# Half-width output tiles on TensorE in a graph-and-experts kernel: the last 53 destinations of an attention layer, and the overflow rows of a mixture of experts

## The chip, the cores and the metric

The kernel runs on one core of one Trainium2 chip. The time is the device time of one execution in microseconds (us). Of the engines, PE is TensorE (matmul; "PEld" is its loading of weights), DVE is VectorE, ACT is ScalarE, POOL is GpSimd and SP issues DMAs. Line numbers (L1273) are those of the kernel before.

## The reference, cut to what matters

There are 3125 nodes with 256 features, 103,125 edges (50,000 pairs in both directions and one loop per node), and four layers, each added to its input after a layer norm:

```python
x = x + gat3(ln(x))          # three graph attention layers: softmax over edges
x = x + moe16(ln(x))         # 16 experts, each token goes to its top 2
x = x + relu(xn @ W + segment_sum((xn @ M)[src], dst))
x = x + moe8(ln(x))          # 8 experts, one per token

# one attention layer of gat3
e = leaky_relu(el[src] + er[dst]); ex = exp(e - max)
out = segment_sum(ex / sum * h[src], dst)

# moe16
top_probs, top_idx = top_k(softmax(x @ gate), 2)
out = sum over the two experts of p * ((silu(x @ w1) * (x @ w2)) @ w3)   # hidden width 512
```

With the fixed inputs the 16 experts of `moe16` get 473, 306, 378, 384, 428, 407, 354, 351, 470, 372, 338, 459, 390, 379, 405 and 356 rows (6250 in all, worked out from the reference). Seven of them have more than 384 rows, and three of those have more than 448.

## The kernel before

All matmuls named here are in fp32. One fp32 matmul of the program shows as two instructions (two passes) in the profile, so counts of PE instructions are twice the matmuls. The Tile scheduler writes each engine's order; it may interleave pieces of neighbouring steps, but an engine works through its own order strictly.

**Attention (`dense_attention`).** The edges are held as a dense table of counts, sources on 128 partitions (25 tiles `s`), destinations along the row. Destinations are worked in 13 groups (`GROUPS`): twelve of 256 and a last one of 53. For each group and each `s`, DVE makes `pm` = max(tau, rho) times the counts (L1270), and PE multiplies it, as the stationary operand, with the node features `h` of that source tile (257 columns, L1273), one matmul for each 128 destinations, summed over `s` in PSUM (`acc`). `pm` has six buffers, so DVE runs up to six tiles ahead. What follows a group is put into a list `later` and issued inside the next group's loop at fixed `s`: `divide` (L1291 to L1300), and then, in layers 1 and 2, `onward` (transposes at L1313, the next layer's projection at L1113). In layer 3 the router follows instead: `norm`, `gate` and `send` (L613 to L674), which end in an indirect DMA that scatters each row to its expert's place in DRAM (`rows`). After the last group the router's `finish` counts each expert's rows and makes a small table of which expert has rows beyond 384, for the next stage.

**First experts (`routed_experts`).** Each of the 16 experts has 384 rows in the main loop: `turn` loads and transposes them (L732, L737), `first` multiplies them by w1 and w2 (weights stationary, 384 rows moving, L762) and makes `hid` = silu times product (L765, L766), and `second` multiplies `hid` by w3 for each 128 rows (L775), scales it (`y`, L778) and adds it into DRAM `sums` by an indirect DMA on POOL (L780). Rows beyond 384 are worked in slots of 128, one slot after each of the experts 3 to 10 (`BETWEEN = 8`), whether a slot has an expert or only the spare tile: `first_more` (transposes L800, matmuls of 128x128 weights with 128 moving rows L807) and `second_more` (L819, scaled at L821, indirect DMA L824). The weights of a slot's expert are loaded again by SP from a table entry that SP reads (L785 to L796), into the same rotating buffers as the main loop's weights. Scatters into `sums` of one expert are free of order among themselves; those of different experts or slots wait for one another. `y` has three buffers. If more slots are needed than `BETWEEN`, a branch at the end works the rest.

**Order at the seams.** The experts' first rows are read only when all scattered rows have landed. `sums` are read back only when the last scatter has landed.

Of the kernel before, what the change touches and what calls it, by code (L numbers as in the profile page):

```python
# [21 lines left out]
P = 128  # L22
N = 3125
NT = 25
# [498 lines left out]
BETWEEN = 8  # L523
# [40 lines left out]
class Router:  # L564
# [115 lines left out]
    def finish(self, cp, pp, over):  # L680
# [11 lines left out]
        nc.vector.tensor_scalar(end[:, 0, NX0:], total, float(EACH * P), None, op0=OP.is_gt)  # L692
        for j in range(4):
            nc.vector.tensor_tensor(end[:, j + 1, NX0:], end[:, j, NX0:], end[:, j, NX0 - (1 << j):-(1 << j)],
                                    op=OP.add)
        end = end[:, 4, NX0:]
        table = self.table
        nc.vector.tensor_scalar(table[:, 2, 0:1], end[:, NX0 - 1:], float(BETWEEN), None, op0=OP.is_gt)
        slot = cp.tile([1, NX0], F32, name="more_slot")
        nc.gpsimd.iota(slot, pattern=[[1, NX0]], base=0, channel_multiplier=0, allow_small_or_imprecise_dtypes=True)  # L700
        done = cp.tile([1, NX0, NX0], BF16, name="more_done")
        nc.vector.tensor_tensor(done, end[:, None, :].to_broadcast([1, NX0, NX0]),
                                slot[:, :, None].to_broadcast([1, NX0, NX0]), op=OP.is_le)
        nc.vector.tensor_reduce(slot, done, AX.X, OP.add)
        nc.vector.tensor_scalar(table[:, 0], slot, float(NX0 - 1), None, op0=OP.min)

        nc.vector.tensor_scalar(slot, slot, float(NP), float(EACH * P), op0=OP.mult, op1=OP.add)
        nc.vector.tensor_scalar(table[:, 1], slot, float(NX0 * NP), None, op0=OP.min)


def routed_experts(tc, x, ident, rows, sums, places, w1, w2, w3, load):
# [10 lines left out]
    with tc.tile_pool(name="rw", bufs=3) as ep, tc.tile_pool(name="rx", bufs=2) as xp, \  # L722
# [46 lines left out]
        def second(e, xs, hid, o):  # L769
            who = xp.tile([P, nq], I32, name="who")  # L770
            nc.gpsimd.tensor_copy(who, xs[:, :, D])
            for q in range(nq):
                ps = po.tile([P, D], F32, name="ps_o")
# [9 lines left out]

        def first_more(slot):
            e = nc.values_load(places[0:1, 0, slot:slot + 1], engines=(mybir.EngineType.SP,), min_val=0,  # L785
                               max_val=NX0 - 1, skip_runtime_bounds_check_because="min with the last expert")
            at = nc.values_load(places[0:1, 1, slot:slot + 1], engines=(mybir.EngineType.SP,), min_val=0,
                                max_val=NX0 * NP, skip_runtime_bounds_check_because="min with the spare tile")
            xs = mp.tile([P, ROW0], F32, name="xs1")
            nc.sync.dma_start(xs, rows[ds(at, P)])  # L790
            a = ep.tile([P, KD, HID0], F32, name="w1")
            nc.sync.dma_start(a, w1[ds(e, 1)].rearrange("o (k p) h -> p (o k) h", p=P))
            b = ep.tile([P, KD, HID0], F32, name="w2")
            nc.sync.dma_start(b, w2[ds(e, 1)].rearrange("o (k p) h -> p (o k) h", p=P))
            o = op_.tile([P, nh, D], F32, name="w3")
            nc.sync.dma_start(o, w3[ds(e, 1)].rearrange("o (k p) f -> p (o k) f", p=P))  # L796
            xsT = mp.tile([P, KD, P], F32, name="xsT1")
            ps = tp.tile([P, KD, P], F32, name="ps_x")
            for k in range(KD):
                nc.tensor.transpose(ps[:, k], xs[:, k * P:(k + 1) * P], ident)  # L800
            nc.scalar.copy(xsT, ps)
            p1 = pp.tile([P, nh, P], F32, name="ps_h1")
            p2 = pp.tile([P, nh, P], F32, name="ps_h2")
            for ps, w in ((p1, a), (p2, b)):
                for j in range(nh):
                    for k in range(KD):
                        nc.tensor.matmul(ps[:, j], w[:, k, j * P:(j + 1) * P], xsT[:, k], start=(k == 0),  # L807
                                         stop=(k == KD - 1))
            hid = mp.tile([P, nh, P], F32, name="hid1")
            for j in range(0, nh, 2):  # L810
                s = sp.tile([P, 2, P], F32, name="silu")
                nc.scalar.activation(s, p1[:, j:j + 2], AF.Silu)
                nc.vector.tensor_tensor(hid[:, j:j + 2], s, p2[:, j:j + 2], op=OP.mult)
            return slot, xs, hid, o

        def second_more(slot, xs, hid, o):
            ps = po.tile([P, D], F32, name="ps_o")
            for j in range(nh):
                nc.tensor.matmul(ps, hid[:, j], o[:, j], start=(j == 0), stop=(j == nh - 1))  # L819
            y = yp.tile([P, D], F32, name="y")  # L820
            nc.vector.tensor_scalar(y, ps, xs[:, D + 1:D + 2], None, op0=OP.mult)  # L821
            who = yp.tile([P, 1], I32, name="who1")
            nc.gpsimd.tensor_copy(who, xs[:, D:D + 1])
            independent(tc, f"more{slot}", nc.gpsimd.indirect_dma_start(  # L824
                out=sums[:, :], out_offset=bass.IndirectOffsetOnAxis(ap=who, axis=0), in_=y, in_offset=None,
                bounds_check=NP + CAP0 - 1, oob_is_err=True, compute_op=OP.add))
# [4 lines left out]
        for e in range(NX0):  # L831
# [5 lines left out]
            more = first_more(e - 3) if 0 <= e - 3 < BETWEEN else None  # L837
            if e + 1 < NX0:
                turned = turn(e + 1)
            second(e, xs, hid, o)  # L840
# [961 lines left out]
```

## Time and profile before

| | us |
|---|---|
| median of 3 runs (1888.27 to 1890.5) | 1888.33 |
| the profiled execution: its own time | 1892.43 |
| its span, first to last instruction | 1890.7 |
| PE busy in the span | 1836.9 (97%) |
| DVE / ACT / POOL busy | 976.8 / 717.0 / 305.1 |
| mean granted TensorE clock | 0.989 |

The profile has a page and several views. In a row of groups, the columns are line, engine, operation, output and inputs with their shapes, count, then busy time in us and the mean of one in ns, and then the idle time of that engine just before, with what released it. For a matmul "128\*53 128x257" is a stationary operand of 128x53 and a moving one of 128x257. In a row of the timeline, the columns are start and length in us, engine, line, operation and count. Matmuls are pipelined, so the length of one (about 0.38 us) is longer than its share of a stream; a stream is better timed from its first start to the next line's start.

The attention layers run from about 72 to 1064 us, the router's end and the first rows to 1083, the first experts from there to 1385.

### The profile page before, as it was taken

The page shows a single profiled execution, that of the slowest core. Times are in us where ns is not written, and L with a number is a line of the kernel's source. Part 1 is how long each engine was busy: PE and PEld are TensorE (multiplying, and loading weights), DVE is VectorE, ACT ScalarE, POOL GpSimd, SP SyncE. Part 2 cuts the span into 40 slices and gives each one's busy share as a digit, 9 for nine tenths or more (in the row PEclk, how much of TensorE's full clock was granted, in tenths as well). Part 3 has the DMA queues.
Part 4 walks back from the last instruction along what each step waited for, and adds up shares of the span by engine and source line. Part 5 has one row for each costly group of instructions (what it writes and reads, how often), then busy time and mean ns, then how long its engine had stood idle before and what let it go on. Part 6 is the DMA issues. An engine that isn't in the chain of part 4 may idle for free. (4 is left out here: it accounts for less than half of the span.)

```text
span 1890.7 us, 27634 instructions
## 1 busy us (share of the span) xinstructions
PE 1836.9 (97%) x9569; PEld 1465.0 (77%) x9569; DVE 976.8 (52%) x2687; ACT 717.0 (38%) x2055; POOL 305.1 (16%) x456
## 2 busy tenths in 40 slices
PE   6999999999999999999999899999989999999997
PEld 4788888887888888788888567777668887555886
DVE  5898888875555555577777522222243222324221
ACT  3767766761011111122222211111138998544221
POOL 4210100000000000133333222323210000122122
PEclk9999999999999999999999899999989999999999
DMA  4111214756000000111111265667430000733664
GB/s 114 32 41 40 71 38 166 292 237 251 1 1 0 1 1 6 41 45 45 46 45 41 91 178 156 213 191 201 104 87 1 1 1 10 246 146 135 220 209 126
DMA packets 104342, 183.08 MB, mean 97 GB/s; under 512 B 10808, under 2 KB 73433, under 8 KB 104160
## 3 DMA queue, kind: packets, MB, share of 16 engines
q1 hardware_dynamic: 72268, 124.31, 19.5%
q0 software_dynamic: 16784, 34.42, 6.7%
q10 hardware_dynamic: 15138, 22.44, 3.7%
q8 instruction: 82, 1.34, 0.3%
q14 instruction: 70, 0.57, 0.1%
HBM read 93.05 MB, written 90.17 MB: 97 GB/s over the span
## 5 line engine op out<-in xcount | busy, mean ns | idle before, releaser
L1273 PE MATMUL acc<-big,pm 128*128 128x257 f32 (+1 forms) x3750 | 863.3, 382 | 1.3 <-DVE pm L1270 1.1
L1273 PEld LDWEIGHTS acc<-big,pm 128*128 128x128 f32 (+1 forms) x3750 | 685.7, 187 | 107.0 <-issue 3.5
L1270 DVE SCALAR_TENSOR_TENSOR pm<-tau,rho,counts 128x256 f32<-128x256 f32 (+1 forms) x975 | 446.2, 470 | 232.5 <-PE acc L1273 227.7
L762 PE MATMUL ps_h<-xsT,w 128*128 128x384 f32 x512 | 167.8, 486 | 0.6 <-ACT xsT L738 0.6
L1392 PE MATMUL acc<-msg,cr 128*128 128x512 f32 (+1 forms) x625 | 157.9, 403 | 0.1
L762 PEld LDWEIGHTS ps_h<-xsT,w 128*128 128x128 f32 x512 | 97.2, 190 | 65.2 <-ACT xsT L738 0.8
L1392 PEld LDWEIGHTS acc<-msg,cr 128*128 128x128 f32 (+1 forms) x625 | 114.7, 185 | 29.2 <-ACT cr L1388 1.2
L1388 ACT ACTIVATE cr<-counts 128x256 fp32r<-128x256 uint8 (+1 forms) x325 | 130.5, 402 | 13.6 <-PE acc L1392 6.7
L1645 ACT CAST counts<-acc_c 128x500 uint8<-128x500 f32 (+1 forms) x155 | 95.9, 677 | 94.6 <-PE acc_c L1635 94.6
L995 PE MATMUL ps_y<-t_wd,hsT 128*128 x480 | 108.8, 380 | 0.3 <-ACT hsT L1023 0.3
L766 DVE TENSOR_TENSOR hid<-silu,ps_h 128x384 f32<-128x384 f32 x64 | 35.5, 554 | 139.2 <-PE ps_h L762 139.2
L765 ACT ACTIVATE silu<-ps_h 128x384 f32<-128x384 f32 x64 | 31.4, 490 | 199.6 <-PE ps_h L762 199.6
L1620 DVE TENSOR_TENSOR ohk<-iota_k,key 128x2016 f16<-128x2016 f16 (+1 forms) x79 | 94.4, 1194 | 22.2 <-PE acc_c L1635 22.1
L995 PEld LDWEIGHTS ps_y<-t_wd,hsT 128*128 128x128 f32 x480 | 88.8, 190 | 11.6 <-ACT hsT L1023 0.5
L780 POOL DMA_INDIRECT sums<-y,who x48 | 74.6, 1554 | 129.5 <-DVE y L778 119.8
L1315 ACT ACTIVATE yT<-ps_m 128x256 f32<-128x256 f32 (+1 forms) x50 | 18.7, 374 | 201.0 <-PE ps_m L1313 200.9
L1614 ACT ACTIVATE ohs<-iota_s,low 128x128 f16<-128x128 f16 x286 | 94.1, 401 | 0.0
L901 PE MATMUL ps_H<-big,t_w 128*128 128x512 f32 (+1 forms) x224 | 93.1, 552 | 0.7 <-ACT H L903 0.5
L775 PE MATMUL ps_o<-w,hid 128*128 128x256 f32 x384 | 86.9, 379 | 0.0
L1635 PEld LDWEIGHTS <-ohs 128*128 128x128 f16 x1250 | 77.7, 98 | 10.9
L1635 PE MATMUL acc_c<-ohk,ohs 128*128 128x125 f16 x1250 | 84.5, 218 | 0.0
L775 PEld LDWEIGHTS ps_o<-w,hid 128*128 128x128 f32 x384 | 71.2, 190 | 8.9
(304 smaller groups left out, 1939.1 us busy)
## 6 DMA issues: line engine op xcount, KB each, us to landing
rows<-empty SPq DMA_DIRECT2D x16, 2564.0 KB, 15.9
w<-in_L_ffn_w_dram ACTq DMA_DIRECT2D x42, 512.0 KB, 7.6
hs<-rows SPq DMA_DIRECT2D x29, 641.0 KB, 4.2
w<-in_L_ffn_w_dram SPq DMA_DIRECT2D x30, 512.0 KB, 4.7
rows<-empty SPq DMA_DIRECT2D x16, 516.0 KB, 5.2
t_wd<-in_L_ffn_Wd_dram SPq DMA_DIRECT2D x8, 1024.0 KB, 11.8
xs<-rows SPq DMA_DIRECT2D x15, 387.0 KB, 5.4
bias<-in_L_ffn_bd_dram SPq DMA_DIRECT2D x30, 128.0 KB
```

Source lines behind the costliest of these rows:

```text
L762: nc.tensor.matmul(ps, w[:, k, j * P:(j + 1) * P], xsT[:, k], start=(k == 0), stop=(k == KD - 1))
L775: nc.tensor.matmul(ps, hid[:, j, q * P:(q + 1) * P], o[:, j], start=(j == 0), stop=(j == nh - 1))
L901: nc.tensor.matmul(ps[:, :n], a[:, k, j * P:(j + 1) * P], xnT[:, k, c:c + n], start=(k == 0), stop=(k == KD - 1))
L995: nc.tensor.matmul(ps, hsT[:, j], d[:, ds(e, 1), j, :].rearrange("p o f -> p (o f)"), start=(j == 0), stop=(j == nh - 1))
L1270: nc.vector.scalar_tensor_tensor(pm[:, :n], tau[:, :n], now.rho[:, s:s + 1], edges[:, s, :n], op0=OP.max, op1=OP.mult)
L1273: nc.tensor.matmul(acc[:r, j, :D + 1], pm[:, q:q + r], now.h[:, s], start=(s == 0), stop=(s == NT - 1))
L1388: nc.scalar.activation(cr[:, :n], edges[:, s, :n], AF.Copy, accum_out=seen[:, a * NT + s:a * NT + s + 1])
L1392: nc.tensor.matmul(acc[:r, j].rearrange("p h d -> p (h d)"), cr[:, q:q + r], msg[:, s].rearrange("p h d -> p (h d)"), start=(s == 0), stop ...
L1614: nc.scalar.activation(far[:, i], self.iota_s, AF.Abs, scale=-1.0, bias=self.low32[:, batch, i:i + 1])
L1620: nc.vector.tensor_tensor(to[:, i:tiles].rearrange("p t (x u) -> p t x u", u=2), iota.rearrange("p (x u) -> p x u", u=2)[:, None].to_broad ...
L1635: nc.tensor.matmul(acc[:, u], ohs[:, i], ohk[:, i, :KEYS], start=(t == 0), stop=(t == TW - 1))
L1645: nc.scalar.copy(to[:, :, d0 % PAIR:d0 % PAIR + whole * WIN].rearrange("p s (u d) -> p u s d", u=whole), acc[:, :whole])
```

## The change

Three things are changed.

1. **Last group.** The 25 matmuls of the last group (53 destinations) write in turn to PSUM partitions 0 to 52 (even `s`) and 64 to 116 (odd `s`). DVE makes the stationary operand for six source tiles at once, in two plain operations (`few`, two buffers), where it made it for one in one fused operation. `divide` then adds the two halves: two ACT copies and two DVE additions more.
2. **Overflow rows.** Slots are of 64 rows, each with its own expert, and are worked two at a time, one on partitions 0 to 63 and one on 64 to 127, after the experts 3, 5, 7, 9 and 11 (`BETWEEN = 5` pairs). The rows are now the stationary operand (64 columns) and the weights move (512 columns). `hid` so comes out with rows on partitions and is transposed by four PE transposes (`turn_more`). Each half is scattered by an indirect DMA of its own, and these no longer carry the mark that frees them of order.
3. **Table and buffers.** The table counts halves (an expert beyond 448 rows takes two), so it has 32 entries. The pair's weights lie in a fixed buffer (`room`), the one that `xnT` of the next layer takes later, and not in the rotating ones.

```diff
+SHARE = P // 2
+SUBS = NX0 * (CAP0 - EACH * P) // SHARE
-BETWEEN = 8
+BETWEEN = 5
...
-        nc.vector.tensor_scalar(end[:, 0, NX0:], total, float(EACH * P), None, op0=OP.is_gt)
+        nc.vector.tensor_scalar(own, total, float(EACH * P + SHARE), None, op0=OP.is_gt)
+        nc.vector.scalar_tensor_tensor(end[:, 0, NX0:], total, float(EACH * P), own, op0=OP.is_gt, op1=OP.add)
...
         def first_more(slot):
...
+            for h, (a, b, o) in enumerate(places_of):
+                k = 2 * slot + h
...
+                nc.sync.dma_start(xs[h * SHARE:(h + 1) * SHARE], rows[ds(at, SHARE)])
...
+                nc.sync.dma_start(a, w1[ds(e, 1)].rearrange("o (k p) h -> p (o k) h", p=P))
...
-            for ps, w in ((p1, a), (p2, b)):
-                for j in range(nh):
-                    for k in range(KD):
-                        nc.tensor.matmul(ps[:, j], w[:, k, j * P:(j + 1) * P], xsT[:, k], start=(k == 0),
-                                         stop=(k == KD - 1))
+            for ps, j in ((p1, 1), (p2, 2)):
+                for k in range(KD):
+                    for of in own:
+                        nc.tensor.matmul(ps[of[0]], xsT[:, k, of[0]], of[j][:, k], start=(k == 0), stop=(k == KD - 1))
+            s = sp.tile([P, HID0], F32, name="silu")
+            nc.scalar.activation(s, p1, AF.Silu)
+            nc.vector.tensor_tensor(s, s, p2, op=OP.mult)
+        def turn_more(slot, xs, s, own):
+            ps = tp.tile([P, nh, P], F32, name="ps_x")
+            for j in range(nh):
+                nc.tensor.transpose(ps[:, j], s[:, j * P:(j + 1) * P], ident)
+            hid = mp.tile([P, nh, P], F32, name="hid1")
+            nc.scalar.copy(hid, ps)
         def second_more(slot, xs, hid, own):
             for j in range(nh):
-                nc.tensor.matmul(ps, hid[:, j], o[:, j], start=(j == 0), stop=(j == nh - 1))
+                for half, _, _, o in own:
+                    nc.tensor.matmul(ps[half], hid[:, j, half], o[:, j], start=(j == 0), stop=(j == nh - 1))
+            for half, *_ in own:
...
-            independent(tc, f"more{slot}", nc.gpsimd.indirect_dma_start(
-                out=sums[:, :], out_offset=bass.IndirectOffsetOnAxis(ap=who, axis=0), in_=y, in_offset=None,
-                bounds_check=NP + CAP0 - 1, oob_is_err=True, compute_op=OP.add))
+                nc.gpsimd.indirect_dma_start(
+                    out=sums[:, :], out_offset=bass.IndirectOffsetOnAxis(ap=who[:SHARE], axis=0), in_=y[:SHARE],
+                    in_offset=None, bounds_check=NP + CAP0 - 1, oob_is_err=True, compute_op=OP.add)
...
-            more = first_more(e - 3) if 0 <= e - 3 < BETWEEN else None
+            more = [first_more((e - 3) // 2)] if e % 2 and 0 <= e - 3 < 2 * BETWEEN else []
...
+                        if n <= P // 2:
+                            if s % SOME == 0:
+                                m = min(SOME, NT - s)
+                                few = sp.tile([P, SOME, n], F32, name="few")
+                                nc.vector.tensor_tensor(few[:, :m], tau[:, None, :n].to_broadcast([P, m, n]),
+                                                        now.rho[:, s:s + m, None].to_broadcast([P, m, n]), op=OP.max)
+                                nc.vector.tensor_tensor(few[:, :m], few[:, :m], edges[:, s:s + m, :n], op=OP.mult)
+                            at = s % 2 * (P // 2)
+                            nc.tensor.matmul(acc[at:at + n, 0, :D + 1], few[:, s % SOME], now.h[:, s], start=(s < 2),
+                                             stop=(s >= NT - 2))
...
+                        if r0 <= P // 2:
+                            both = sp.tile([P, D], F32, name="y1")
+                            nc.scalar.copy(both[:r0], acc[P // 2:P // 2 + r0, 0, :D])
+                            nc.scalar.copy(col[:r0, 1:], acc[P // 2:P // 2 + r0, 0, D:D + 1])
+                            nc.vector.tensor_tensor(both[:r0], acc[:r0, 0, :D], both[:r0], op=OP.add)
+                            nc.vector.tensor_tensor(col[:r0, 1:], weight, col[:r0, 1:], op=OP.add)
```

## The prediction

> **What bounds the kernel now.** First the page: PE is busy for 97% of the span, so a matmul saved counts in full wherever PE's queue does not then wait for something else. The edits lie in two stages. For the last attention groups I read the timeline of PE around the end of layer 1:
>
> ```profile
> 439.72 10.72 PE L1273 MATMUL acc<-big,pm 128*128 128x257 f32 x48
> 450.37 0.44 PE L1313 MATMUL ps_m<-ident,y 128*128 128x128 f32 x2
> 450.74 1.07 PE L1273 MATMUL acc<-big,pm 128*53 128x257 f32 x4
> 451.74 1.14 PE L1113 MATMUL ps_m<-we,yT 128*128 128x258 f32 x4
> 452.81 0.64 PE L1273 MATMUL acc<-big,pm 128*53 128x257 f32 x2
> 453.38 0.44 PE L1313 MATMUL ps_m<-ident,y 128*128 128x128 f32 x2
> 453.75 1.07 PE L1273 MATMUL acc<-big,pm 128*53 128x257 f32 x4
> 454.75 1.14 PE L1113 MATMUL ps_m<-we,yT 128*128 128x258 f32 x4
> 455.82 4.55 PE L1273 MATMUL acc<-big,pm 128*53 128x257 f32 x20
> 460.30 0.43 PE L1221 MATMUL ps_m<-ident,lr 128*128 128x128 f32 x2
> ```
>
> PE has no gap here. The last group has 25 matmuls, 50 passes; 30 stand in the 53-wide rows, so 20 of the first row's 48 are its own too, and they begin at 450.37 - 20 x 0.214 = 446.1 (10.72 / 48 is 0.22 a pass, 0.214 without the tail of the last). The group with its guests takes 460.3 - 446.1 = 14.2 us, of which its own 25 matmuls are 50 x 0.214 = 10.7. A pass of 257 columns is 0.214 us whether 128 or 53 wide: half the array idles.
>
> For the overflow slots I read the same view for expert 3:
>
> ```profile
> 1142.24 0.38 PE L800 MATMUL ps_x<-ident,xs 128*128 128x128 f32 x2
> 1143.22 3.73 PE L807 MATMUL ps_h<-xsT,w 128*128 128x128 f32 x32
> 1151.87 1.89 PE L819 MATMUL ps_o<-w,hid 128*128 128x256 f32 x8
> ```
>
> No gaps again. The first `y` of an expert (L778, DVE timeline) comes at 1148.62 and 1170.29, 21.67 apart with a slot, and at 1334.39 and 1350.55, 16.16 apart without: a slot costs 5.51 us, eight cost 44.1. (Seven have rows.)
>
> **Do half-width tiles overlap?** Everything hangs on this, and the trace has a nearest row: L910 writes fp32 products 32 wide to four strips of partitions in turn.
>
> ```profile
> 1660.74 1.92 PE L910 MATMUL ps_zT<-H,t_wg 128*32 128x512 f32 x16
> ...
> 1662.59 1.09 PE L945 MATMUL ps_rows<-ident,H 128*128 128x128 f32 x8
> ...
> 1670.87 9.61 PE L901 MATMUL ps_H<-big,t_w 128*128 128x512 f32 x22
> ```
>
> L901 shows 9.61 / 22 = 0.437 us for a pass of 512 columns. Sixteen such passes in turn would take 7.0; L910's sixteen take 1662.59 - 1660.74 = 1.85. In tenths of a us, four passes are in flight from 1660.7 and eight overlap at 1661.2: four waves of 0.43. So strips do run together, both passes of fp32 too.
>
> Here a page speaks against it. The Trainium skill, "TensorE: Matmul & The Clock Gate", Part 3, says that a weight load overlaps running matmuls only where the row group differs; halves of columns share their rows. By that rule each wave would bare at least one load, and L1273's 53-wide load has a mean of 0.127 us: 3.3 us for the 26 waves of a group, 2.0 for the 16 of a pair of slots. The same page's strict FIFO would also keep a half's second pass between the two halves. L910 contradicts both as a price: its loads (eight in the first 0.16 us) leave no gap between its waves. I go by the row; by the rule the sum below would be -7 instead of -23 (two layers 2 x 1.8, layer 3 1, slots 5 x 8.4 instead of 44.1).
>
> **Last group, layers 1 and 2.** Twenty-five matmuls become 13 turns of two passes: 26 x 0.214 = 5.6 instead of 10.7, -5.1. In the new PE order the blocks between guests are of 10, 3, 4 and 8 matmuls, which pair to 5 + 2 + 2 + 4 = 13, so nothing more is lost. The Trainium skill, "TensorEngine Tiling (Array Packing)", Key Properties, says that a change of tiling mode drains PE, which speaks against short blocks. The rows above price it: four 53-wide passes take 451.74 - 450.74 = 1.00 where four full ones take 0.87, about 0.15 a change; eight changes, but they are there before too (53 wide among 128 wide), so they cost nothing new.
>
> Is DVE quick enough? Before, 25 operations of 0.27. After, five pairs of plain ones; from L1270 (256 elements 486 ns, 53 elements 274, so 1.04 ns an element over 219) 318 elements are 0.55, together about 4.9 us against 6.9. With two `few` buffers the first twelve tiles are ready before the group starts (both batches stand ahead of `divide` in DVE's order). The third batch stands behind `divide` (1.4 us from 446.19 to about 447.6), so its end is about 2.6 us into the group; PE reaches it at 12 x 0.214 + 0.5 for the transposes = 3.1. Covered by 0.5; without that cover each us late costs one. The last one-tile batch stands on DVE behind the guests' two L1116; it ends some 0.6 before PE needs it. The two ACT copies and two DVE additions (0.36 + 0.2, 0.42 + 0.15) fall in the next layer's first group, before its tenth tile; the tile's `h` is needed at `s` = 24. Nothing. Two layers: -10.2.
>
> **Last group, layer 3.** Here the chain is DVE's, not PE's:
>
> ```profile
> 1063.69 0.19 PE L658 MATMUL ps_z<-g_sel,before 128*128 128x32 bf16 x1
> ...
> 1063.99 0.64 PE L1273 MATMUL acc<-big,pm 128*53 128x257 f32 x2
> ...
> 1067.15 0.41 DVE L626 TENSOR_SCALAR row<-big,g_mv,g_rstd 128x256 f32<-128x256 f32 x1
> ...
> 1074.01 0.23 DVE L667 TENSOR_TENSOR g_to<-g_tf,off 128x1 int32<-128x1 f32 x2
> ```
>
> The last matmul stands behind L658, the ranking of the tiles before, which waits for DVE. When PE's group shrinks, that group's `gate` and `send` are no longer inside it but after: in the new order the last tile's L626 stands behind the previous pair's L667. Counted from the group's start at 1051.0: gate sums at 9.3 (before 9.1), about 24 dependent DVE steps of 0.21 to L667 at 14.3, row at 14.5 where it was 16.1. So about 1.5 of the 5.1 stays, less some ACT table loads (1.28 each) that now fall in the chain: between 0 and -3, I take -1. Later edits in `finish` (the table with 512 instead of 256 elements, some 1.5 us more of DVE) stand behind L667 and lie under the 7.7 us of warming matmuls and the first rows' DMA.
>
> **Overflow pairs.** A pair's PE work: two transposes 0.23; 8 matmuls of 512 columns, 16 passes in 8 waves of 0.427, 3.41; four new transposes 4 x 0.115 = 0.46; 8 matmuls of 256 columns, 8 waves of 0.213, 1.71; four new mode changes 0.6. Sum 6.4, five pairs 32.0. Removed 44.1. So -12.1. The waits for silu, product, transposes and copy have 6 and 4 of the expert's own w3 matmuls (2.56 and 1.7 us) between them in PE's order, against about 1.0 and 0.9 needed: covered. If that cover were gone, some 2 us a pair.
>
> SP: a pair issues eight DMAs (3 MB) and four table reads where a slot had four and two; ten halves instead of eight slots are 3 MB more in all. The queue behind them is the next experts' rows. The stage moves up to 420 GB/s, so a pair needs about 8 us, and it is issued an expert and a half (over 20 us) ahead, since `room` is free. At the start, 0.5 MB goes ahead of expert 1's weights (1.3 us of over 10 spare). Nothing.
>
> **POOL and the scatters.** This is the doubtful place:
>
> ```profile
> 1153.57 1.55 POOL L780 DMA_INDIRECT sums<-y,who  x1 [0.30 <-issue]
> 1161.87 1.55 POOL L824 DMA_INDIRECT sums<-y,who  x1 [6.75 <-DMA sums<-y,who]
> ...
> 1171.52 1.56 POOL L780 DMA_INDIRECT sums<-y,who  x1 [7.78 <-DVE y L778]
> ```
>
> A slot's scatter waits for the landing of the expert's last, 8.3 us after its start while weights pour in (5.7 to 6.1 in the experts without slots, 2.5 the least). After, two halves follow each other so: last scatter 21.3 us after the expert's start, first half at 29.6, second at about 37, landed by about 41.5 when the burst is over. Behind the second stand the even expert's scatters, whose `y` is there at 35: late by 6, but the next pair's are due only at 55.7 and those land by 51, so the lateness does not add up. `y`'s three buffers do bind: the even expert's third `y` waits for the second half's landing, 41.5 where it is due at 38.5; DVE stands for 3 us, and behind it `hid` of the next expert, which PE needs at about 45 (two PSUM pairs ahead). Cover about 2 to 3 us. I take 0; up to 3 us a pair, 15 in all, for the range.
>
> **Sum.** -10.2 - 1 - 12.1 = -23.3 on the profiled execution, 1892.43 (its span 1890.7 and 1.7 around it) to 1869.1. The median of the runs is 4.1 below the profiled one; the same saving from 1888.33 gives 1865.0.
>
> **Rivals.**
> - *The pairs take turns (slower).* If 64-wide halves do not overlap, a pair of slots is 0.23 + 6.83 + 0.46 + 3.41 + 0.6 = 11.5, five 57.7 against 44.1, +13.6, and the attention part gives 0: 1902. With a share f of the overlap the sum is 13.6 - 25.6 f - 11.2 f; it turns to a gain from f = 0.37. Against it: L910. For it: nothing but that no 64-wide row exists. 7%.
> - *The scatter chain comes through, or loads show.* Stalls of 1 to 3 us a pair by the three `y` buffers, or some tenths of a us at each wave: 5 to 15 back, about 1875. For it: the 8.3 us landings; against it: bursts are shorter than a pair's two experts. 20%.
> - *Attention keeps its time.* If the guests' transposes and ACT's copies (short now against a 5.6 us group) hold PE, only the slots gain: 1888.3 - 12.1 = 1876. For it: layer 3; against: each guest has a block of matmuls before it. 8%.
> - *Not what it says.* The counts give 2+1+1+2+2+1+1 = 10 halves, just `2 * BETWEEN`; an eleventh would open the branch, some 150 us. The expert at exactly 384 rows lacks a further row by a logit gap of 0.0003, far over fp32 error. 1%.
>
> **How the numbers follow.** The likeliest case, 64%, has 1860 to 1870. The two partial ones, 28%, lie at 1870 to 1882. The range 1858 to 1880 leaves out the slower rival, the branch and the far end of stalls, some 16%. Under 0.2% (3.8 us, about what a measurement here can tell) needs f near 0.4: 3%. Slower, with the branch, 8%; faster 89%.
>
> **What would show it.** L1273's successor 53 wide with 50 passes a group in about 5.6 us of starts; L800 to L819's successors busy in about 6 us a pair; first `y` of odd and even experts about 22.6 and 16.2 apart; L778 waiting for a DMA of `sums` if the chain binds; layer 3's L667 only about a us sooner. Wrong if the two halves' passes start one after the other.

## The result, and the profile after

The changed kernel takes 1863.73 us (median of 4, 1861.74 to 1866.04) where the kernel before, run beside it, takes 1889.29 (4 runs): ratio 0.9865, 95% interval 0.9848 to 0.9882, or 25.6 us less. The prediction was 1865.0, range 1858 to 1880. The profiled execution took 1866.04, its span is 1864.3 where it was 1890.7. Line numbers from here on are those of the changed kernel: the matmul of a last group is L1306, that of the other groups L1313, a pair's first products L828, its transposes L837, its second product L846.

The timeline of PE around the end of layer 1, after (start and length in us, operation, count of passes):

```profile
445.87 2.38 PE L1306 MATMUL acc<-big,few 128*53 128x257 f32 x20
448.19 0.44 PE L1361 MATMUL ps_m<-ident,y 128*128 128x128 f32 x2
448.55 1.07 PE L1306 MATMUL acc<-big,few 128*53 128x257 f32 x6
449.55 1.14 PE L1142 MATMUL ps_m<-we,yT 128*128 128x258 f32 x4
450.53 0.38 PE L1361 MATMUL ps_m<-ident,y 128*128 128x128 f32 x2
450.84 1.08 PE L1306 MATMUL acc<-big,few 128*53 128x257 f32 x8
451.85 1.14 PE L1142 MATMUL ps_m<-we,yT 128*128 128x258 f32 x4
452.92 1.95 PE L1306 MATMUL acc<-big,few 128*53 128x257 f32 x16
454.80 0.43 PE L1250 MATMUL ps_m<-ident,lr 128*128 128x128 f32 x2
456.29 8.95 PE L1313 MATMUL acc<-big,pm 128*128 128x257 f32 x40 [1.06 <-DVE pm L1310]
```

The group with its guests (the matmuls of the step before that are set between its own) runs from 445.87 to 454.80, 8.93 us where it was 14.2 by the prediction's count and 14.4 from its first own pass in the trace (445.89). Twenty passes take 448.19 - 445.87 = 2.32, ten turns of 0.214 and an end: two passes at a time. A turn is one pass in each half, side by side. From the transposes (L1250) to the next layer's first group it is about 1.5 us, as before the change; now PE waits 1.06 of them for the mask `pm`, where it waited 0.68 for a `y` of L1300.

The same view at the first pair of slots, after:

```profile
1130.33 0.38 PE L821 MATMUL ps_x<-ident,xs 128*128 128x128 f32 x2
...
1131.83 3.65 PE L828 MATMUL ps_h<-big 128*64 128x512 f32 x16
...
1138.39 0.60 PE L837 MATMUL ps_x<-ident,silu 128*128 128x128 f32 x4
...
1140.65 1.95 PE L846 MATMUL ps_o<-big,hid 128*64 128x256 f32 x16
```

The first `y` of the odd experts around pairs come at 1136.87, 1175.65, 1214.44 and 1253.22, so two experts with a pair take 38.78 us. Two without take 2 x 16.16, so a pair costs 6.46 (6.4 predicted), where a slot of 128 cost 5.51. So a pair is dearer than a slot; the gain is that five pairs do what eight slots did, and the overlap is what keeps a pair cheap enough for that. The stage from the first `y` to the last went from 1385.7 - 1096.4 = 289.3 us to 1361.9 - 1084.4 = 277.5: 11.8 less.

Where the 26.4 us of the span went, from the starts of the same lines in both timelines: the last group of layer 3 begins 10.15 earlier (layers 1 and 2; before it began at about 1051.0, counted back by passes), the first rows' transposes 11.8 earlier (layer 3: 1.7), the last `y` 23.7 earlier (the pairs: 11.9), and the end 26.4 earlier. The last 2.7 lie after the experts, where nothing was edited.

Layer 3 ends in DVE's chain now as before. In the timeline of PE:

```profile
1046.28 1.50 PE L1306 MATMUL acc<-big,few 128*53 128x257 f32 x10
...
1053.40 0.21 PE L660 MATMUL ps_z<-g_sel,before 128*128 128x32 bf16 x1 [3.73 <-DVE g_sel L656]
...
1055.39 0.69 PE L633 MATMUL ps_x<-ident,row 128*128 128x128 f32 x2 [1.61 <-DVE row L628]
...
1060.72 0.20 PE L660 MATMUL ps_z<-g_sel,before 128*128 128x16 bf16 x1 [3.15 <-DVE g_sel L656]
```

Before, the first of these rankings (L658 there) lay inside the last group, ahead of its last matmul. Now it lies behind the whole group, and PE stands 3.73 us for it.

The scatter chain makes DVE wait as foretold. In the timeline of DVE:

```profile
1200.62 0.48 DVE L792 TENSOR_SCALAR y<-ps_o,xs 128x256 f32<-128x256 f32 x1 [4.09 <-DMA sums<-y,who]
1201.02 0.55 DVE L778 TENSOR_TENSOR hid<-silu,ps_h 128x384 f32<-128x384 f32 x1
```

An even expert's third `y` waits 4.09 us for the landing that frees a `y` buffer, and `hid` of the next expert stands behind it. PE begins that expert's first products at 1197.58 and gets through 20 passes of them (6.61 us by the same row elsewhere) before it needs this `hid`, so at 1204.2; it is there at 1201.6. The cover that is left here is 2.6 us. In a second profile of the same kernel (`after_again` below, where this expert's first products begin at 1154.40) it is less:

```profile
1158.77 0.48 DVE L792 TENSOR_SCALAR y<-ps_o,xs 128x256 f32<-128x256 f32 x1 [5.41 <-DMA sums<-y,who]
```

This `y` comes 4.37 us after the first products where the other came 3.04 after, so the cover left is 1.3 us.

### The profile page after: what moved, and what is told of

The parts are those of the page before. It is cut to its first block, busy times and chain, and to the rows that moved or that the text cites. A ratio compares the mean times of both kernels' runs of the same rounds, so it can differ in the third digit from the quotient of the medians.

```text
span 1864.3 us, 27270 instructions
## 1 busy us (share of the span) xinstructions
PE 1808.2 (97%) x9423; PEld 1427.1 (77%) x9423; DVE 971.2 (52%) x2644; ACT 717.5 (38%) x2052; POOL 309.6 (17%) x461
## 3 DMA queue, kind: packets, MB, share of 16 engines
q1 hardware_dynamic: 74060, 127.06, 20.2%
## 5 line engine op out<-in xcount | busy, mean ns | idle before, releaser
L1313 PE MATMUL acc<-big,pm 128*128 128x257 f32 x3600 | 828.1, 382 | 3.1 <-DVE pm L1310 3.1
L1313 PEld LDWEIGHTS acc<-big,pm 128*128 128x128 f32 x3600 | 667.6, 190 | 94.6 <-DVE pm L1310 4.8
L1310 DVE SCALAR_TENSOR_TENSOR pm<-tau,rho,counts 128x256 f32<-128x256 f32 x900 | 427.5, 487 | 211.1 <-PE acc L1313 203.5
L774 PE MATMUL ps_h<-xsT,w 128*128 128x384 f32 x512 | 168.4, 487 | 0.6 <-ACT xsT L750 0.6
L774 PEld LDWEIGHTS ps_h<-xsT,w 128*128 128x128 f32 x512 | 96.8, 190 | 66.9 <-issue 1.9
L1436 ACT ACTIVATE cr<-counts 128x256 fp32r<-128x256 uint8 (+1 forms) x325 | 130.5, 402 | 14.4 <-PE acc L1440 6.9
L789 PE MATMUL ps_o<-w,hid 128*128 128x256 f32 x384 | 87.2, 379 | 0.0
L1683 PEld LDWEIGHTS <-ohs 128*128 128x128 f16 x1250 | 77.7, 98 | 10.9
L789 PEld LDWEIGHTS ps_o<-w,hid 128*128 128x128 f32 x384 | 71.0, 190 | 8.8
## 6 DMA issues: line engine op xcount, KB each, us to landing
t_wd<-in_L_ffn_Wd_dram SPq DMA_DIRECT2D x8, 1024.0 KB, 11.9
```

What stands on the lines that cost most here:

```text
L774: nc.tensor.matmul(ps, w[:, k, j * P:(j + 1) * P], xsT[:, k], start=(k == 0), stop=(k == KD - 1))
L789: nc.tensor.matmul(ps, hid[:, j, q * P:(q + 1) * P], o[:, j], start=(j == 0), stop=(j == nh - 1))
L1310: nc.vector.scalar_tensor_tensor(pm[:, :n], tau[:, :n], now.rho[:, s:s + 1], edges[:, s, :n], op0=OP.max, op1=OP.mult)
L1313: nc.tensor.matmul(acc[:r, j, :D + 1], pm[:, q:q + r], now.h[:, s], start=(s == 0), stop=(s == NT - 1))
L1436: nc.scalar.activation(cr[:, :n], edges[:, s, :n], AF.Copy, accum_out=seen[:, a * NT + s:a * NT + s + 1])
L1683: nc.tensor.matmul(acc[:, u], ohs[:, i], ohk[:, i, :KEYS], start=(t == 0), stop=(t == TW - 1))
```

## The experiments

The kernels ran in three groups, each on one chip beside the kernel before. It took 1888.9 us beside the kernels with one edit, without alternation and with two `y` buffers, 1890.36 beside those with one `y`, five buffers, the first early `tau` and all three, and 1889.57 beside the last four (blocks of eight, no batches, the second early `tau`, and the changed kernel again). So the changed kernel itself stood beside the last group alone, with 1862.73 us; for the others its 1863.73 is taken, measured where the kernel before took 1889.29. Runs of one kernel differ by 4 us, and by up to 8 (two `y` buffers: 1878.24 to 1886.69), so of small differences the trace is asked and not the median.

### One edit at a time

The first kernel has only the attention edit, the second only the slots.

> The kernel before with the attention edit alone: last groups of 53 in two halves, the overflow slots as they were. My theory: 13 turns of two passes for 25 matmuls of two, so 5.1 us in each of layers 1 and 2 and about 1 (measured in the changed kernel: 1.7) in layer 3: 11 to 12 us faster than before, and the experts' stage as before (a slot 5.51 us, first y of two neighbouring experts 21.67 apart with a slot). The rival that attention keeps its time: 0. The rival that something after the experts moved with the layout: part of the 2.7 us there stays in this kernel too, so 13 to 14.

> The changed kernel with the attention edit undone: overflow slots of 64 in pairs, last groups as before. My theory: a pair 6.4 to 6.5 us, five of them instead of eight slots of 5.51, so 11.8 to 12.1 us faster than before; the two edits lie in different stages and add up, so this run's gain and that of the kernel with attention alone make the whole 25.6 but for what lies after the experts (2.7). If that 2.7 belongs to the pairs (what they leave to the later stage: scatters, memory), it shows here: 14 to 15. The rival that the pairs cost more than slots: slower by 13.

Attention alone took 1878.32 us (ratio 0.9944, 0.9927 to 0.996): 10.6 less. Slots alone took 1876.77 (0.9934, 0.9917 to 0.9951): 12.1 less. In the first the experts' stage is as before (first to last `y` 1375.0 - 1085.6 = 289.4), in the second it is 277.5. So each edit gives its own term, in its own stage, and the rival by which attention keeps its time falls. The sum is 22.7, 2.9 short of the 25.6 of both together; each of these has an interval of about 3 us to either side. From the last `y` to the end, where nothing was edited, the profiles have 505.0 us before, 502.4 after, 502.3 with attention alone, 503.3 with slots alone. With either edit alone the stretch is shorter than in the one profile before, so the 2.7 us can't be put down to one of them.

### Whether it is the overlap

Besides the overlap, the changed kernel has fewer DVE operations a group, and five pairs where there were eight slots. To keep all of that and take the overlap away, the halves do not alternate:

```diff
-                            at = s % 2 * (P // 2)
+                            at = s // 13 * (P // 2)
...
-                for k in range(KD):
-                    for of in own:
+                for of in own:
+                    for k in range(KD):
                         nc.tensor.matmul(ps[of[0]], xsT[:, k, of[0]], of[j][:, k], start=(k == 0), stop=(k == KD - 1))
...
-            for j in range(nh):
-                for half, _, _, o in own:
+            for half, _, _, o in own:
+                for j in range(nh):
                     nc.tensor.matmul(ps[half], hid[:, j, half], o[:, j], start=(j == 0), stop=(j == nh - 1))
```

> The changed kernel with the same instructions in another order: the halves no longer alternate. In a pair all eight matmuls of one half come before those of the other (twice: the first two products, and the second one), and in the last attention groups the tiles 0 to 12 go to the lower half, 13 to 24 to the upper. My theory is that the gain is overlap of neighbouring passes in different halves of the array: without it a pair costs 11.5 instead of 6.46 us (five: +25) and the last group of layers 1 and 2 10.7 instead of 5.6 (+5 each), layer 3 +1 to +2: about 36 us slower than the changed kernel, 11 slower than before, some 1900. If the gain came from something else (fewer slots' fixed parts, fewer DVE operations), or if the chip overlaps passes that stand further apart, the time stays within 5 us of the changed kernel.

In the first products of a pair this edit does less than the text above says: it puts two matmuls (four passes) of one half ahead of two of the other, and that twice. All of one half first, it has in the second product and in the attention groups.

It took 1885.05 (18 runs, ratio 0.998, 0.9973 to 0.9988): 21.3 slower than the changed kernel, not 36. The timeline of PE of this kernel, layer 1 and then the first pair:

```profile
442.40 4.55 PE L1306 MATMUL acc<-big,few 128*53 128x257 f32 x20
...
458.47 8.95 PE L1313 MATMUL acc<-big,pm 128*128 128x257 f32 x40 [1.22 <-DVE pm L1310]
...
1144.50 3.70 PE L828 MATMUL ps_h<-big 128*64 128x512 f32 x16
...
1153.37 2.86 PE L846 MATMUL ps_o<-big,hid 128*64 128x256 f32 x16
```

Attention lost its overlap whole: the twenty passes are all of one half and take 4.55 us (the upper half's first stands behind guests of full width), and from the group's start to the next layer's first pass it is 458.47 - 442.40 = 16.07 against 10.42, 5.65 in each of the two layers (15.9 before the change). Layer 3 lost as much: from the group's start to the warming matmuls behind the chain (L557, whose results nothing uses) 1074.48 - 1048.69 = 25.8 against 1061.64 - 1040.85 = 20.8, 5.0 where I had expected 1 to 2. The pair lost little: L828 not at all (3.70 against 3.65), L846 0.91, five pairs 4.7. The sum, 11.3 + 5.0 + 4.7 = 21.0, is the time found.

So attention has no gain without the overlap, with the batches and all else of the edit in place. My sum for the pair was wrong for two reasons: the edit moved less than I had said, and in L828 four passes of one half stand ahead of four of the other, and yet they ran together.

### How far ahead PE reaches

> The changed kernel with the two first products of a pair in another order: four matmuls (eight passes of 512 columns) of the lower half, then four of the upper. With the halves in turn in blocks of four passes these sixteen took no longer (3.70 us against 3.65), while the second product in blocks of eight (256 columns) took 2.86 against 1.95: as though PE's queue ran four passes ahead of a busy half. If it is a count of passes, the sixteen take 12 waves of 0.427 and a start of 0.24, 5.4 us; if it is a time (0.85 us, the four passes of 256), they run two passes ahead: 14 waves, 6.2 us; if overlap is complete, 3.7; if none, 7.1. By the first, 1.7 us a pair and 8.5 in all slower than the changed kernel.

The edit puts the four matmuls of the lower half (both products, eight passes of 512 columns) ahead of the four of the upper. The sixteen took 5.42 us, and the kernel 1875.04 (0.9924, 0.9907 to 0.994). The experts' stage is 286.3 us, 8.8 longer, where 8.5 was expected; the median is 12.3 above the changed kernel beside it, the profiled execution 8.4 (1870.64 against 1862.22). The trace in slices of one pass shows how, L828 alone, in slices of about 0.43 us (the columns are length, PE's busy time and the passes that fall into the slice, the same of the weight loads, then the granted clock, the DMA share and GB/s):

```profile
1127.57:1128.00 0.43, 0.43 (x1) 0.19 (x2) 1.00 0.88 338
1128.00:1128.42 0.42, 0.42 (x2) 0.14 (x1) 1.00 0.05 15
...
1128.85:1129.28 0.43, 0.43 (x2) 0.14 (x1) 1.00 0.85 300
1129.28:1129.71 0.43, 0.43 (x3) 0.19 (x3) 1.00 1.00 376
1129.70:1130.13 0.43, 0.43 (x4) 0.19 (x2) 1.00 0.81 314
1130.13:1130.56 0.43, 0.43 (x4) 0.19 (x2) 1.00 0.30 114
1130.56:1130.99 0.43, 0.43 (x4) 0.14 (x1) 1.00 0.00 0
1130.99:1131.41 0.42, 0.42 (x3) 0.14 (x1) 1.00 0.00 0
1131.41:1131.84 0.43, 0.43 (x2) 0.14 (x1) 1.00 0.00 0
```

A slice with one stream shows two passes (one that ends, one that begins), a slice with two streams four. One stream runs for four slices, two for four, one for four: the upper half's first pass starts when the lower half's fifth does, in all five pairs (1.77 us after the first pass). That is 12 waves, the count of four passes as expected, and not a time: with 256 columns it was four passes as well (2.86 us; there the upper half's first starts 0.92 us in, the lower half's fifth 0.91), with 512 four again. It is not the end of a sum in PSUM either: the lower half's first sum ends after four passes here, after eight in the case of 256 columns. So PE does not work through its order strictly, as was said of all engines at the start. What was not tried is whether it is four passes or two fp32 matmuls, and whether the number changes with the halves' width or with more than two strips.

### How much cover the scatter chain has

> The changed kernel with two y buffers in the experts' stage instead of three. It tests the cover of the scatter chain, which the prediction took as 2 to 3 us a pair: DVE's third y of an even expert waits 3.2 to 4.1 us for a landing, and no gap shows on PE. With two buffers that y waits for the scatter after, 2 to 4 us more: if the cover was nearly used up, PE stalls 1 to 4 us a pair, 5 to 20 us slower than the changed kernel. If the cover is much larger than I said, the same time within 2 us.

Two `y` buffers instead of three took 1882.14 us (0.9958, 0.9941 to 0.9974), 18.4 more than the changed kernel: more than the slots had gained. In the timeline of PE of this kernel:

```profile
1160.77 6.61 PE L774 MATMUL ps_h<-xsT,w 128*128 128x384 f32 x20
1170.52 5.58 PE L774 MATMUL ps_h<-xsT,w 128*128 128x384 f32 x12 [3.14 <-DVE hid L778]
```

and of its DVE:

```profile
1164.56 0.48 DVE L792 TENSOR_SCALAR y<-ps_o,xs 128x256 f32<-128x256 f32 x1 [6.56 <-DMA sums<-y,who]
1169.52 0.48 DVE L792 TENSOR_SCALAR y<-ps_o,xs 128x256 f32<-128x256 f32 x1 [4.48 <-DMA sums<-y,who]
```

The third `y` comes 8.75 us after the start of L774 (1169.52 - 1160.77), in the changed kernel 3.04 (1200.62 - 1197.58): 5.7 later, less the 2.6 of cover, is 3.1, and PE waits 3.14. So the chain of DVE, POOL and landings is as the prediction drew it, and three buffers stand 2.6 us (1.3 in the second profile) from the point where it begins to cost. PE's four waits are 11.5 us (3.14, 2.51, 3.56, 2.25), but the experts' stage is 296.9, 19.4 longer. Of the rest a part is the clock. The stretches around the first wait (length, busy time and count of PE, of its loads, of DVE, ACT and POOL, then the granted clock, the DMA share and GB/s):

```profile
1167.40:1170.50 3.10, 0.00 (x0) 0.00 (x0) 0.98 (x3) 0.00 (x0) 1.59 (x2) 0.93 0.78 91
1170.50:1173.40 2.90, 2.88 (x5) 1.67 (x6) 0.43 (x1) 0.49 (x1) 1.34 (x1) 0.50 0.71 152
1173.40:1177.00 3.60, 3.60 (x17) 2.44 (x16) 1.11 (x2) 1.14 (x3) 0.19 (x1) 0.99 0.37 53
```

Behind the wait PE runs at half clock, from 1170.0 to 1173.4. Two experts with a pair take 1188.14 - 1144.51 = 43.63 us between the same L774, 4.85 more than 38.78: 3.14 of waiting and 1.71 for 3.41 us at half clock. Three of the four waits are followed by such a stretch, 5.1 us. With 11.5 that makes 16.6 of the 19.4. The stage's last `y` itself waits 2.91 us for a landing and comes 7.05 us after its expert's first pass of L789 where it came 5.38 after, 1.7 more; the last 1.1 I have not placed.

Why three and not four? The three slow stretches begin 44.4 us apart, 13 times 3.41, as if on a fixed grid of 3.41 us. Along that grid, these are the slice ahead of the third slow stretch and the later one of the two over the fourth wait (columns as above):

```profile
1255.39:1258.80 3.41, 0.63 (x2) 0.49 (x3) 1.41 (x3) 0.49 (x1) 1.12 (x2) 1.00 0.49 59
1299.76:1303.17 3.41, 2.00 (x6) 1.25 (x7) 1.75 (x4) 0.49 (x1) 1.56 (x1) 1.00 0.67 129
```

PE was busy for 0.74, 0.90 and 0.63 us of the slices ahead of the three slow stretches; the fourth wait lies across two slices, which have 2.56 and 2.00. So it seems to be PE's busy share of such a slice that counts, and not the length of a wait. The other profiles agree. In the fourteen of this text, each divided along its own grid from 25 us on, all 85 slices with PE busy for less than 0.4 of them are followed by a slow one. Of the slices at full clock, 19 of the 66 with 0.4 to 0.7 are, and ten of the 7289 with 0.7 or more, all ten near 118 us. Why those ten stays open.

### Fewer buffers taken

> The changed kernel with both halves' y of a pair in one tile, made by one DVE operation: four y buffers taken per two experts with a pair where it was five. If the scatter chain costs PE nothing, as I hold, the waits of DVE's y shrink (3 to 4 us at the even experts' third y) and the time stays the same within 1 us. If the chain does cost something in the experts' stage, 1 to 5 us faster.

With one tile and one DVE operation for both halves' `y`, the waits of `y` for landings went from 19.2 us (8 of them; 25.7 and 9 in the second profile) to 8.3 (3). The time is 1865.23 (0.9868, 0.9851 to 0.9884), the experts' stage 277.5: the same. So these waits of DVE, under PE's cover, cost nothing, and as a buffer against slower landings the edit is free.

### The batches of masks

> The changed kernel without its batches: the last groups make their masks one tile at a time in one fused operation, as before the change, and keep the two halves. 25 operations of 0.27 are 6.9 us of DVE against 5.6 of PE, with guests' matmuls (3.4 us) between. Theory: PE then waits for DVE at the end of the group, up to 1 us in layers 1 and 2, and 0 to 1 in layer 3: 0 to 3 us slower than the changed kernel. If the batches don't matter: the same within 1.

It took 1868.59 (0.9885, 0.9868 to 0.9901), 5.9 more than the changed kernel beside it. From the first pass of attention to the experts' first `y` it is 1087.6 - 72.0 = 1015.6 us, where the changed kernel has 1012.4 and, in its second profile, 1011.8: 3.2 to 3.8, a little above what was expected, and for another reason. In layer 1 the group with its guests takes 456.06 - 445.71 = 10.35 instead of 8.93, and PE shows no wait in it. It is in pieces: with 25 DVE operations instead of ten, the guests fall elsewhere among the matmuls. The blocks are of 7, 1, 2, 3, 3 and 9 matmuls, so 15 turns instead of 13 (2 x 0.43) and two blocks more, with four changes of width more (0.15 each by the prediction's row): 1.46 together, and 1.42 are found. So the batches are worth about 3.5 us of the 12 that attention gained, through the order of PE: they keep the turns full. The prediction had costed them as DVE's cover only.

### Five buffers in layer 3

> The changed kernel with five few buffers instead of two in layer 3 alone, so that all batches of the last group may be made ahead of the gate's chain of small DVE steps. In the changed kernel PE stands 9.2 us in all for that chain in layer 3. Theory: the batches between the steps are part of the chain, 0.55 us each, so 1 to 2 us faster. Rival: the chain is the gate's own steps alone, and PE's group merely moves ahead: 0.

It took 1866.72 (0.9867, 0.9844 to 0.989). From the first pass of attention to the first `y` of the experts it has 1084.5 - 72.0 = 1012.5 us, the changed kernel 1012.4. The rival is nearly right. From the last group's start to the warming matmuls it is 20.2 us against 20.8 (20.2 also in the kernel with all three edits below): 0.6, the length of one batch operation, and not 1 to 2. The rest of layer 3's chain is the router's own small steps.

### The gap between the layers

The next layer's first `tau` is made behind the last group in the changed kernel. Two edits put it into the group, the first between tiles 17 and 18, the second between 16 and 17. The second (the first has `TERMS`, which is 18, where this has `TERMS - 1`):

```diff
-                    tau = tau_next if a else terms(now, 0)
+                    tau = tau_next if a or i else terms(now, 0)
...
+                        if s == TERMS - 1 and a + 1 == len(GROUPS) and nxt:
+                            tau_next = terms(nxt, 0)
```

> The changed kernel with one edit: the first tau of the next layer is made in the middle of the last group instead of behind it, as it is for the other groups. At the two layer boundaries PE stands 1.06 us for pm behind tau in the changed kernel (1.5 from the end of the transposes to the first pass). My theory: these gaps go, 1 to 1.5 us each, 2 to 3 us faster than the changed kernel. Rival: the sums that it transposes then stand in the way of the shorter group, whose few tiles come later on DVE by as much: 0.

> The changed kernel with the next layer's first tau made ahead of the last group's tile 17 (not behind it: an odd number of matmuls ahead of the transposes left one without a partner, a turn of 0.43 us). The gap of 1.49 us at the two boundaries should go whole: by the trace 1.0 to 1.2 us each, 2 to 2.5 in all faster than the changed kernel in the same call.

> The three edits together on the changed kernel: tau early, one y a pair, five few buffers in layer 3. They lie in different stages, so their gains should add: 3 to 5 us faster than the changed kernel, about 1859 to 1861. If only the early tau helps: 2 to 3.

The first took 1864.61 (0.9865, 0.9848 to 0.9883), the three edits together 1863.76 (0.9854, 0.9838 to 0.9871). The changed kernel has 0.9865, so the 3 to 5 us expected of the three did not come; by the trace (first pass of attention to the experts' first `y`) they have 1010.4 against 1012.4. In the first the wait for `pm` is gone, but the stretch from the last group's start to the next layer's first pass is 451.92 - 442.07 = 9.85 us against 10.42: 0.57 instead of 1.5. Tile 17 now stood alone between two guests, a turn of 0.43 us with half the array idle. With `tau` a tile earlier, in the timeline of PE (the lines are numbered two higher there):

```profile
446.97 1.14 PE L1142 MATMUL ps_m<-we,yT 128*128 128x258 f32 x4
447.95 0.38 PE L1250 MATMUL ps_m<-ident,lr 128*128 128x128 f32 x2
448.26 1.95 PE L1308 MATMUL acc<-big,few 128*53 128x257 f32 x16
450.13 8.95 PE L1315 MATMUL acc<-big,pm 128*128 128x257 f32 x40
```

The stretch is 450.13 - 440.99 = 9.14, 1.28 less at each boundary, and from the first pass of attention to the experts' first `y` it is 1077.2 - 68.0 = 1009.2 against 1011.8 in the changed kernel beside it. The medians are 1861.64 (0.9855, 0.9838 to 0.9871) and 1862.73, whose ranges overlap. So this version is 2.6 us better by the trace, and the times cannot tell it from the changed kernel.

### What lies where nothing was edited

> The changed kernel itself, beside the three others of this call on the same chip: 1863 to 1866 us. If what it gained after the experts (2.7 us, where nothing was edited) is only where the clock's half-speed windows fell, stretches without edits differ by such windows between this profile and the first one, too.

It took 1862.73 (0.9864, 0.9848 to 0.9881). Its profiled span is 1860.5 us, 3.8 less than the 1864.3 of the first, and the 3.8 us are there before attention begins (first pass at 68.2 against 72.0). The stretches of the two profiles (columns as above), the first one:

```profile
30.00:37.00 7.00, 4.37 (x22) 3.07 (x21) 4.30 (x19) 6.93 (x17) 2.33 (x3) 1.00 0.00 0
37.00:44.00 7.00, 6.38 (x21) 4.74 (x20) 3.52 (x8) 3.05 (x11) 2.58 (x2) 0.51 0.01 2
```

and the second:

```profile
30.00:37.00 7.00, 4.38 (x22) 3.19 (x22) 3.72 (x14) 6.38 (x17) 2.66 (x2) 1.00 0.01 2
37.00:44.00 7.00, 6.47 (x46) 5.57 (x47) 5.98 (x11) 5.29 (x17) 4.73 (x2) 1.00 0.00 0
```

The program is the same, the clock is not: 6.8 us at half speed in one, none in the other. The other profiles bear it out: the eight that have such a stretch near 37 us reach attention's first pass at 71.5 to 72.4, the six without it at 68.0 to 68.5. After the experts the kernel before has 0.51 over ten microseconds:

```profile
1395.00:1405.00 10.00, 5.96 (x15) 4.17 (x16) 6.74 (x30) 2.54 (x9) 0.00 (x0) 0.51 0.88 280
```

and the changed kernel 0.50 over 6.8:

```profile
1371.70:1378.50 6.80, 3.76 (x10) 2.33 (x10) 5.32 (x24) 1.62 (x6) 0.00 (x0) 0.50 0.99 315
```

That is 3.4 us more at half clock before the change, 1.7 us. But a later stretch is longer in the changed kernel (6.8 us from 1713.0, where before there are 3.4 from 1739.9) and takes 1.2 back. The remaining 2 us lie in the last experts: from their first transposes (tile `ps_cols`) to the end it is 142.3 us before and 140.4 in the changed kernel; the other profiles have 140.4 to 142.2 for it. From the last `y` to the end they have 501.6 to 503.9; the 505.0 before is the highest, in one profile. So the 2.7 is for the most part within what profiles of this program differ by, and its cause stays open.

## Why the prediction was right

- *The overlap.* Right, and it is the cause in attention: with the same matmuls in another order 16.3 us go there, more than the 12 gained, since layer 3 keeps the new order that costs it some 3 us (below). In the pairs it is seen directly (3.65 us for sixteen passes that would take 6.83 in turn), and where four waves of it are taken away the sixteen take 5.42. The rival by which pairs take turns gave 11.5 us a pair; it measured 6.46. The rule of the Trainium skill weighed in the prediction ("TensorE: Matmul & The Clock Gate", Part 3: a load is hidden only where the row group differs) would have made the sum -7; the loads stayed hidden, as the nearest row had said. (The same part also lets a load go ahead into a background buffer of weights; the prediction passed that over, and no run here tells which it is.) It also says that matmuls start and end strictly in program order. For two halves the slices above show otherwise: the ninth pass starts with the fifth.
- *Layers 1 and 2, -10.2.* The next layer's first pass comes 5.5 earlier in layer 1 (461.79 to 456.29), 10.15 in both (at the start of layer 3's last group). The 13 turns and the blocks of 10, 3, 4 and 8 are there as drawn. The changes of width were miscounted: before there were five blocks and ten changes, not eight, so two go in each layer, 0.3 us, which with 5.1 makes the 5.4 to 5.5 of the stretches (15.90 to 10.42, 15.84 to 10.41). Some 0.7 of the 10.9 is lost again elsewhere in attention, so that the term of 10.2 is met to a tenth is luck: two misses cancel.
- *Layer 3, -1 (0 to -3).* 1.7. The order that the prediction read is the reason: the ranking moved from inside the group to behind it. How large both sides are, the run without overlap shows: with the new order and a group of full length the stretch from the group's start to the warming matmuls is 25.8 us, with overlap 20.8, and before it was 22.9 (about 1051.0, counted back by passes, to 1073.85). So the shorter group gives 5.0, and the rest of the edit, the order above all, takes some 3 back. The -1.7 is smaller than 22.9 - 20.8 because the first rows are now waited for (0.84 us, where it was 0.19).
- *Pairs, -12.1.* -11.8, a pair 6.46 against 6.4.
- *Scatter chain, 0 (up to 15).* 0, and the drawing was right: the third `y` waits up to 4.09 us in one profile and 5.41 in the other where I had worked out 3, and 2.6 and 1.3 us of cover are left where I said 2 to 3. One buffer less costs 18.4 us, so the doubt was in the right place, on the other side of the edge, and the edge is nearer than the first profile shows.
- *Mis-sized.* The sum of -23.3 became -25.6 (medians). The terms of the stages add to 10.15 + 1.7 + 11.9 = 23.7; what the sum missed lies behind the experts, 2.7 us in one pair of profiles, where the prediction had no term; no run gives the change a part in it, and its cause stays open. The batches of masks, about 3.5 us of attention's gain, were in the sum only by the blocks read from the order, not as a term.

## What to carry to other kernels

Where a matmul's output is 64 partitions or narrower, let consecutive matmuls write to two halves: the second half then costs little (sixteen passes of 512 columns in 3.65 us, eight waves of 0.427 being 3.42), and one row of the trace with narrow outputs was enough to see it beforehand. A half-width unit need not be cheaper than a full one, if fewer of them do the work. Count the turns block by block, since a guest behind an odd number of matmuls leaves a turn half empty (0.43 us here). Where PE is the bound, also work out how far the others' chains stand from showing: a chain of scatters with 1.3 to 2.6 us of cover cost nothing, and the same with one buffer less cost 18 us, about a quarter of them because a wait of 3 us can be followed by a stretch of slow clock.

## What the runs showed of the hardware

- PE runs ahead of a busy half: passes for the other half start while up to four passes of the first, which come earlier in the program, have not yet started. Blocks of four passes a half cost nothing (3.70 against 3.65 us for sixteen passes of 512 columns), blocks of eight lose four waves (5.42). Where guests of full width stand between the halves there is no gain (4.55 us for twenty passes of 257, against 2.38).
- A change between matmuls of half and of full width costs about 0.15 us: in the prediction's rows four passes 53 wide and the change behind them take 1.00 us where four full passes take 0.87, and four changes and two turns more make 1.42 us in the kernel without batches (1.46 by this price).
- A wait of PE has a second price. After waits of 2.51, 3.14 and 3.56 us the granted clock was 0.50 for 3.41 us, which adds 1.7; after one of 2.25 it was not. All stretches at half clock that end within these profiles are 3.4, 6.8, 10.2 or 13.7 us long; the Trainium skill has the same step ("TensorE: Matmul & The Clock Gate", Part 1: a free-running window of about 3.4 us in which PE's activity decides the clock). That part warns of gaps of over some 3.4 us; here 2.51 was enough, in a slice of which PE was busy for 0.90 us. Whether such a stretch falls at 37 us or not made 3.8 us between two executions of the same kernel, which is most of their spread.
